# The prologue of a convolution, attention and expert kernel: group norm, first block and setup products in another order

## The chip, the cores and the metric

The kernel runs on one core of one Trainium2 chip. The metric is device microseconds of one execution; lower is better. Of the kernel before there are three timed runs and one profiled execution.

## The reference

The input x is (4, 128, 64, 64), four images of 128 channels and 4096 places. Two layers follow each other.

- Layer 0: x is normalised in 32 groups of 4 channels (group norm). Three 1x1 convolutions with bias and PReLU give e1 and e2 (64 channels each) and asm (128 channels). Scores are e1 transposed times e2, 4096 x 4096 per image; softmax over the second axis; the weighted sum of asm is added to x.
- Layer 1: with the places as tokens, layer norm, then attention with queries, keys and values of 128 features, added; then layer norm and a routed expert layer (64 experts, each takes its 8 top tokens by a softmax over the tokens; pooled, two dense layers with an exact GELU, scattered back), added.

The core of what concerns the change:

```python
xn = (g - m) / jnp.sqrt(s + eps)                  # mean, variance over 4 channels and all places
e1, e2, asm = prelu(w @ xn + b)                   # w1 64x128, w2 64x128, wa 128x128
out = softmax(e1.T @ e2, axis=2) @ asm.T          # per image
```

## The kernel before, in words

An image is held as 128 partitions (channels) x 4096 columns and is worked in 8 blocks of 512 columns (NB = 8, BLK = 512). Attention takes one block of 512 queries as a row (8 rows), and in each row 8 groups (NG = 8) of four key chunks of 128, that is one block of keys per group.

**PSUM** has 8 banks, in three pools: `sc` (scores, two tiles of two banks), `av` (products, two tiles of one bank, av0 and av1), `ms` (everything else, two tiles of one bank, taken in turn).

**Order of the work.** Instructions are traced by Python and then ordered on each engine by a scheduler, which takes the earlier traced first among those that it holds to be ready. `tc.keep_in_program_order` pins an instruction behind the one traced before it on its engine; `tc.no_sync_barrier` keeps the order between what is traced ahead of it and after it. Work that goes beside attention is written as generators, and a step of a generator (`next`) is traced after each group. `keep_busy(k)` traces k pinned matmuls of the identity into a spare PSUM tile (filler, so that TensorE does not stand idle); `FIRST_FILL` has the counts of the prologue.

**The prologue, in traced order** (function `tile_unshifted`):

1. Lines 118 to 152: the first image's 8 blocks are loaded, four by the SP queue and four by the ACT queue, then the small parameters on the same two queues (a12, wa, ba, aa on ACT; the others on SP). Lines 154 to 181: GpSimd builds the identity and averaging matrices; `avg_g` takes the mean of a group, `off_g` subtracts it.
2. Line 1221: `first_a`, 25 fillers. Lines 1222 and 1223: the first product of `weights_qk` (L503) and its copy on ACT (L505), the first ACT instruction that needs a table.
3. `group_norm(0, first_x)`: eight bn_stats (L220), bn_aggr (L223); then a channel's deviation from its group's mean and the mean itself by two matmuls into one bank (L230, L231); DVE copies both and forms the squared deviation plus the channel's variance (L233 to L237); a third matmul averages that (L240). `inv_sqrt` (L185) adds eps on DVE, takes the power -1/2 on GpSimd (L191) and does one Newton step with three DVE instructions (L192 to L196). Fillers `first_b` stand before the third matmul. Then come the other products of `weights_qk` with `first_e` and `first_c`.
4. `conv(0, first_x)`, a generator. First `normed` (L291) gives xk of block 0. Then, for block n: `both` (L378, pe: e1 and e2 together; L380, pa: asm by four 128-column pieces), ACT adds the bias (ye, L330), PReLU on DVE (te, L283, and L285), the next block's `normed`, and a yield; DVE adds ba (L363), PReLU into the values (L283, L285), and two yields. For block 0 the query and the keys are written in place by three L285 instructions, and ACT copies the query to the other 64 partitions (L344). For the other blocks the keys are placed by two DMAs of the SP queue (L348), and e1 goes to memory (L349).
5. Two `next` of that generator are traced before two setup products: `pgate` (L1239, copied to gate by L1240) and the transposes of a bias, `pw` (L1244, copied to w1bT by L1248). Both take a tile of the `ms` pool, as pe and pa do. `first_d` fillers stand between.
6. `stage(0, 0, ..., ahead=first_conv, pace=(4, 3))`: four more `next` of the convolution, then the attention of image 0. In the first row, after each group, three `next` are traced (so one block).

**A step of attention** (`attention`, L587 to 655): for group g the score matmuls (L625; 64 rows of the array each, the two halves of a key pair on different rows), exp on ACT (L634), the products of the group before (`rows_products`, L559) and the sum of exps on DVE (L646, L649).

Of the kernel before, what the change touches and what calls it, by code (L numbers as in the profile page):

```python
# [9 lines left out]
F32 = mybir.dt.float32  # L10
AF = mybir.ActivationFunctionType
# [15 lines left out]
def tile_unshifted(  # L27
# [91 lines left out]
    for n in range(NB):  # L119
        part = bass.ts(n, BLK)  # L120
        (nc.sync, nc.scalar)[n % 2].dma_start(out=first_x[:, part], in_=x[0][:, part])

    def const_load(name, shape, src, queue=None, pool=None):
        t = (pool or const).tile(shape, F32, tag=name, name=name, bufs=1)
        (queue or nc.scalar).dma_start(out=t, in_=src)
        return t
# [58 lines left out]
    def inv_sqrt(dst, var, eps, k, name):  # L185

        v = small.tile([P, SUB], F32, tag="iv", name=f"{name}_v")
        y = small.tile([P, SUB], F32, tag="iy", name=f"{name}_y")
        z = small.tile([P, SUB], F32, tag="iz", name=f"{name}_z")
        nc.vector.tensor_scalar(v[:, :k], var, eps, None, op0=ALU.add)  # L190
        nc.gpsimd.tensor_tensor(y[:, :k], v[:, :k], mhalf[:, :k], op=ALU.pow)  # L191
        nc.vector.tensor_mul(z[:, :k], y[:, :k], y[:, :k])  # L192
        nc.vector.scalar_tensor_tensor(
            z[:, :k], in0=z[:, :k], scalar=-0.5, in1=v[:, :k], op0=ALU.mult, op1=ALU.mult
        )
        nc.vector.scalar_tensor_tensor(  # L196
            dst, in0=z[:, :k], scalar=1.5, in1=y[:, :k], op0=ALU.add, op1=ALU.mult
        )
# [4 lines left out]
    def group_norm(b, first=None):  # L203
        st = prep.tile([P, NB, 6], F32, tag="gn_st", name=f"gn_st{b}")

        def pair(i):
            if i == NB // 2:
                return []
            if first is not None:
                return [first[:, bass.ts(2 * i + h, BLK)] for h in range(2)]  # L210
            return [
                load_block("xs", x_of(b, 2 * i + h), f"g{b}_{2 * i + h}", 4) for h in range(2)
            ]

        coming = pair(0)
        yield
        for i in range(NB // 2):
            blocks, coming = coming, pair(i + 1)
            for h in range(2):
                nc.vector.bn_stats(out=st[:, 2 * i + h, :], in_=blocks[h])  # L220
            yield
        mv = prep.tile([P, 2], F32, tag="gn_mv", name=f"gn_mv{b}")
        nc.vector.bn_aggr(out=mv, in_=st.rearrange("p n s -> p (n s)"))  # L223
        yield
        ab = const.tile([P, 2], F32, tag=f"gn{b}", name=f"gn{b}")
        if first is None:
            yield from group_norm_turned(b, mv, ab)
            return
        pm = ms_tile(f"gn_pm{b}")
        nc.tensor.matmul(pm[:, 0:1], lhsT=off_g, rhs=mv[:, 0:1], start=True, stop=True)  # L230
        nc.tensor.matmul(pm[:, 1:2], lhsT=avg_g, rhs=mv[:, 0:1], start=True, stop=True)  # L231
        d = prep.tile([P, 2], F32, tag="gn_d", name=f"gn_d{b}")
        nc.vector.tensor_copy(d[:, 0:1], pm[:, 0:1])  # L233
        nc.vector.scalar_tensor_tensor(
            d[:, 1:2], in0=d[:, 0:1], scalar=d[:, 0:1], in1=mv[:, 1:2], op0=ALU.mult, op1=ALU.add
        )
        nc.vector.tensor_copy(ab[:, 0:1], pm[:, 1:2])  # L237
        yield
        pv = ms_tile(f"gn_pv{b}")
        nc.tensor.matmul(pv[:, 0:1], lhsT=avg_g, rhs=d[:, 1:2], start=True, stop=True)  # L240
        inv_sqrt(ab[:, 1:2], pv[:, 0:1], GN_EPS, 1, f"gn{b}")
        gn[b] = ab
        yield
# [42 lines left out]
                o, in0=part(y), scalar=0.0, in1=part(t), op0=ALU.max, op1=ALU.add  # L286
            )

    def normed(b, xb, name):
        xn = block_tile("xn", name)  # L290
        nc.vector.tensor_scalar(  # L291
            xn, xb, gn[b][:, 0:1], gn[b][:, 1:2], op0=ALU.subtract, op1=ALU.mult
        )
        return xn

    keys, values, queries, resid = {}, {}, {}, {}
# [7 lines left out]
    def conv(b, whole=None, cols=None):  # L304
# [9 lines left out]
            return whole[:, bass.ts(n, BLK)]  # L314

        xb = block(0)
        coming = normed(b, xb, f"xk{b}_0")
        xb = block(1)
        yield
        for n in range(NB):  # L320
            xn = coming
            pe = ms_tile(f"pe{b}_{n}")
            if cols:
                for part in cols:
                    nc.tensor.matmul(pe[part, :], lhsT=w12[:, part], rhs=xn, start=True, stop=True)  # L325
            else:
                pa = ms_tile(f"pa{b}_{n}")
                both(xn, pe, pa)
            y, t = block_tile("ye", f"ye{b}_{n}"), block_tile("te", f"te{b}_{n}")
            nc.scalar.activation(y, pe, AF.Identity, bias=b12)  # L330
            places = [kA[h * CR : (h + 1) * CR, bass.ts(n, SUB // 2), :] for h in range(2)]

            def chunks(h):
                return lambda z: z[CR:, :].rearrange("c (p h t) -> c p h t", h=2, t=P)[:, :, h, :]

            if whole is not None and n == 0:

                queries[b, 0, n] = q = block_tile("q", f"e1_{b}_{n}")
                prelu(
                    [(q[:CR, :], lambda z: z[:CR, :])]  # L340
                    + [(places[h], chunks(h)) for h in range(2)],
                    y, t, a12,
                )
                nc.scalar.copy(q[CR:, :], q[:CR, :])  # L344
            else:
                prelu([(y, lambda z: z)], y, t, a12)
                for h in range(2):
                    nc.sync.dma_start(out=places[h], in_=chunks(h)(y))  # L348
                nc.sync.dma_start(out=e1[b][n], in_=y[:CR, :])  # L349
            if n + 1 < NB:  # L350
                coming = normed(b, xb, f"xk{b}_{n + 1}")
            yield
            if cols:
                pa = ms_tile(f"pa{b}_{n}")
            for s in range(SUB if cols else 0):
                for part in cols:
                    nc.tensor.matmul(  # L357
                        pa[part, bass.ts(s, P)], lhsT=xn[:, bass.ts(s, P)][:, part], rhs=wa,
                        start=True, stop=True,
                    )  # L360
            y2, t2 = block_tile("ye", f"ya{b}_{n}"), block_tile("te", f"ta{b}_{n}")
            y3 = y2.rearrange("p (s c) -> p s c", c=C)
            nc.vector.tensor_tensor(  # L363
                y3, pa.rearrange("p (s c) -> p s c", c=C),
                ba.unsqueeze(1).to_broadcast([P, SUB, C]), op=ALU.add,
            )
            prelu(
                [(vT[:, bass.ts(n, SUB), :], lambda z: z.rearrange("p (s c) -> p s c", c=C))],
                y2, t2, aa,
            )  # L370
            if n + 2 < NB:
                xb = block(n + 2)
            yield
            yield

    def both(xn, pe, pa):

        nc.tensor.matmul(pe, lhsT=w12, rhs=xn, start=True, stop=True)  # L378
        for s in range(SUB):
            nc.tensor.matmul(  # L380
                pa[:, bass.ts(s, P)], lhsT=xn[:, bass.ts(s, P)], rhs=wa, start=True, stop=True
            )
# [116 lines left out]
    def weights_qk():  # L499
        wT = []  # L500
        pqk = sc_tile("pwq_pwk")
        for i, w in enumerate((wqT, wkT)):
            nc.tensor.matmul(pqk[:, i, :P], lhsT=w, rhs=unfold, start=True, stop=True)  # L503
            t = block_tile("te", f"wT{i}")[:, :P]
            nc.scalar.copy(t, pqk[:, i, :P])  # L505
            wT.append(t)
# [638 lines left out]


    FILL = (3, 0, 3, 3, 15, 4, 2, 3)
    FIRST_FILL = (25, 3, 2, 2, 2)

    def keep_busy(k, name, t=None):  # L1150

# [66 lines left out]
    nc.sync.dma_start(out=w1b, in_=a["weight1"][:, D1 - 1, :])  # L1218
    cent = block_tile("ye", "cent")[:, :P]
    nc.gpsimd.tensor_scalar(cent, ident, -1.0 / C, None, op0=ALU.add)  # L1220
    keep_busy(FIRST_FILL[0], "first_a")
    projections = weights_qk()
    next(projections)
    first_norm = group_norm(0, first_x)
    for step in range(NB // 2 + 4):
        next(first_norm, None)
        if step == NB // 2 + 2:
            keep_busy(FIRST_FILL[1], "first_b")
    next(projections)
    keep_busy(FIRST_FILL[4], "first_e")  # L1230
    next(projections)
    keep_busy(FIRST_FILL[2], "first_c")
    tc.no_sync_barrier()
    run(projections)
    first_conv = conv(0, first_x)
    next(first_conv)
    next(first_conv)
    pw = ms_tile("pgate")
    nc.tensor.matmul(pw[:, :E], lhsT=cent, rhs=gate, start=True, stop=True)  # L1239
    nc.scalar.copy(gate, pw[:, :E])  # L1240
    keep_busy(FIRST_FILL[3], "first_d")
    pw = ms_tile("pw")
    for c in range(NHC):
        nc.tensor.transpose(  # L1244
            pw[:, bass.ts(c, E)], w1b.rearrange("e (p c) -> e c p", c=NHC)[:, c, :],
            ident[:E, :E],
        )
    nc.scalar.copy(w1bT.rearrange("p c e -> p (c e)"), pw[:, : NHC * E])  # L1248
    run(query(0, 0, 0))
    tc.no_sync_barrier()  # L1250

# [90 lines left out]
                load_part(0, 0, 1, 3, 1)  # L1342
                load_part(1, 1, 1, 2, 1)

    stage(0, 0, chain(group_norm(1), conv(1)), (1, 0), ahead=first_conv, pace=(4, 3))
    packing = pack_weights()
    stage(1, 0, chain(group_norm(2), attn_keys(0), mix_values(0)), (0, 1))
    stage(0, 1, chain(group_norm(3), conv(2, cols=SCORE_COLS[1])), (2, 0), skip=1)
# [743 lines left out]
```

## Time and profile before

| | us |
|---|---|
| median of 3 runs (lowest to highest) | 3227.67 (3226.14 to 3229.38) |
| the profiled execution | 3227.37 |
| its span | 3225.6 |
| TensorE busy in the span | 3200.6 |
| first image's transfers landed | 9.01 |
| first pe matmul starts | 14.41 |
| first score matmul starts | 19.39 |
| first product (av) starts | 27.21 |
| last group of the first row with a projection: its pe starts | 60.00 |

Times within the span count from its start. A profile's chain lists, in order of time, the work that ended last and what released each piece: start, duration, engine, tile and line. A timeline lists instructions by start, with the engine's idle time before them and what ended it. TensorE's records are pipelined: the durations of two that follow each other overlap.

A steady group without a projection beside it takes 1.72 us for eight score matmuls and 3.43 us for sixteen products. A group with one takes 1.06 (pe), 0.89 (pa), 1.92 and 3.43.

### The profile page before, as it was taken

What the parts mean: (1) busy time and instruction counts of PE and PEld (TensorE: products, weight loads), DVE (VectorE), ACT (ScalarE), POOL (GpSimd) and SP (SyncE); (2) the same over time, 40 slices, a digit from 0 to 9 for tenths busy, and PEclk for the clock granted to TensorE, in tenths of its full rate; (3) what the DMA queues carried; (4) which work ended last, traced back from release to release, by engine and by line L of the source; (5) the groups of instructions that cost most, each with busy time, mean ns of one, the idle gap of its engine ahead of it and who ended that gap; (6) DMA issues with size and microseconds to landing.
All of it is one profiled execution on the core that took longest, in us unless ns stands there. A gap on an engine that the chain in (4) does not pass through costs nothing.

```text
span 3225.6 us, 49325 instructions
## 1 busy us (share of the span) xinstructions
PE 3200.6 (99%) x19620; PEld 1574.1 (49%) x19620; DVE 2127.5 (66%) x4237; ACT 1275.0 (40%) x1571; POOL 386.8 (12%) x422
## 2 busy tenths in 40 slices
PE   9999999999999999999999999999999999999997
PEld 5444444444555544444554444444445454546663
DVE  7665577556675668755775657775776566676564
ACT  3344444443433345443333334444333333343341
POOL 0111113210000003240000001332100002010001
PEclk9999999999999999999999999999999999999999
DMA  3121244223232212311221111231131111122159
GB/s 91 49 53 30 76 104 121 77 87 86 73 86 82 63 49 47 79 33 27 53 47 27 37 30 40 78 79 25 44 70 37 37 24 37 24 69 93 34 182 387
DMA packets 370128, 222.90 MB, mean 69 GB/s; under 512 B 275424, under 2 KB 300128, under 8 KB 366560
## 3 DMA queue, kind: packets, MB, share of 16 engines
q1 hardware_dynamic: 365616, 208.51, 24.1%
q10 hardware_dynamic: 3760, 10.10, 0.8%
q8 instruction: 156, 2.56, 0.3%
q0 software_dynamic: 512, 1.05, 0.1%
q14 instruction: 84, 0.69, 0.1%
HBM read 159.75 MB, written 97.19 MB: 80 GB/s over the span
## 4 chain that ended last, share of the span: by engine, by line
PE 98%; DVE 1%; DMA 0%; issue 0%; ACT 0%; SPq 0%; DVEq 0%; POOL 0%; ACTq 0%
PE ps L625 41%; PE av L559 27%; PE av L587 24%; PE pq L528 1%; PE pv L772 1%; PE pe L378 1%; PE po L1457 0%; PE pa L380 0%; PE pa L357 0%; PE pe L325 0%; PE ph L1423 0%; PE pg L828 0%; PE px L1537 0%; DMA first_x<-in_x_dram 0%; PE av_pht L1434 0%; DVE w L1544 0%
## 5 line engine op out<-in xcount | busy, mean ns | idle before, releaser
L634 ACT ACTIVATE pt<-ps 128x1024 f32<-128x1024 f32 x1024 | 1020.9, 1023 | 1466.3 <-PE ps L625 1390.3
L625 PE MATMUL ps<-q,t 128*64 128x512 f32 x4096 | 934.3, 592 | 0.0
L559 PE MATMUL av<-pt,asm 64*128 64x512 f32 x4096 | 922.3, 589 | 0.0
L649 DVE TENSOR_TENSOR sacc<-sacc,pt 128x1024 f32<-128x1024 f32 x448 | 587.3, 1311 | 294.2 <-ACT pt L634 269.7
L587 PE MATMUL av<-pt,tt 128*64 128x256 f32 x3072 | 636.2, 379 | 0.0
L559 PEld LDWEIGHTS av<-pt,asm 64*128 64x128 f32 x4096 | 401.0, 187 | 479.1 <-issue 477.8
L573 DVE TENSOR_TENSOR tt<-pt 128x512 f32<-128x512 f32 x512 | 354.7, 693 | 354.0 <-ACT pt L634 336.5
L625 PEld LDWEIGHTS ps<-q,t 128*64 128x64 f32 x4096 | 305.1, 137 | 482.4 <-issue 451.7
L587 PE MATMUL av<-tt,mixed 128*64 128x256 f32 x2048 | 525.6, 379 | 0.0
L587 PEld LDWEIGHTS av<-pt,tt 128*64 128x64 f32 x3072 | 356.0, 137 | 270.3 <-issue 135.0
L625 PE MATMUL ps<-e,e 64*128 64x512 f32 x2048 | 486.1, 592 | 0.0
L625 PEld LDWEIGHTS ps<-e,e 64*128 64x128 f32 x2048 | 196.2, 187 | 235.8 <-issue 232.6
L587 PE MATMUL av<-tt,tt 128*64 128x256 f32 x1024 | 304.7, 379 | 0.0
L587 PE MATMUL av<-pt,mixed 128*64 128x256 f32 x1024 | 304.6, 379 | 0.0
L587 PEld LDWEIGHTS av<-tt,mixed 128*64 128x64 f32 x2048 | 280.5, 137 | 8.8
L191 POOL TENSOR_TENSOR l_y<-l_v,mhalf 128x4 f32<-128x4 f32 x64 | 64.9, 1013 | 1631.6 <-DVE l_v L190 1631.2
L574 DVE TENSOR_TENSOR pt<-tt,pt 128x256 f32<-128x256 f32 x512 | 219.9, 430 | 17.0
L575 DVE TENSOR_TENSOR tt<-pt 128x256 f32<-128x256 f32 x512 | 219.5, 429 | 17.0
L587 PEld LDWEIGHTS av<-pt,mixed 128*64 128x64 f32 x1024 | 140.2, 137 | 65.4 <-DVE pt L574 0.3
L587 PEld LDWEIGHTS av<-tt,tt 128*64 128x64 f32 x1024 | 140.1, 137 | 4.7 <-DVE tt L575 0.3
L666 POOL TENSOR_TENSOR u<-u,c 128x512 f32<-128x512 f32 x32 | 40.7, 1271 | 555.6 <-ACT c L665 555.6
L646 DVE TENSOR_TENSOR sacc<-pt,pt 128x1024 f32<-128x1024 f32 x32 | 39.1, 1221 | 53.1 <-ACT pt L634 53.1
(323 smaller groups left out, 1755.4 us busy)
## 6 DMA issues: line engine op xcount, KB each, us to landing
wp<-in_weight_dram SPq DMA_DIRECT2D x128, 256.0 KB, 4.2
w<-wp SPq DMA_DIRECT2D x10, 1024.0 KB, 13.5
w<-wp SPq DMA_DIRECT2D x17, 512.0 KB, 9.1
xq<-in_x_dram SPq DMA_DIRECT2D x32, 256.0 KB, 3.9
rb<-inv SPq DMA_DIRECT2D x32, 256.0 KB, 3.3
xT<-xt SPq DMA_DIRECT2D x128, 64.0 KB, 2.2
ak<-xT SPq DMA_DIRECT2D x32, 256.0 KB, 3.6
t<-kt SPq DMA_DIRECT2D x128, 64.0 KB, 2.2
```

Source lines behind the costliest of these rows:

```text
L191: nc.gpsimd.tensor_tensor(y[:, :k], v[:, :k], mhalf[:, :k], op=ALU.pow)
L378: nc.tensor.matmul(pe, lhsT=w12, rhs=xn, start=True, stop=True)
L559: nc.tensor.matmul(avs[b, 0, n][r], lhsT=values[b, 0][rows, j, :], rhs=pt[rows, h, :], start=(j == 0), stop=(j == NJ - 1),)
L573: nc.vector.tensor_sub(tt[:, 0:2, :], p4[:, :, 1, :], p4[:, 0, :, :])
L574: nc.vector.tensor_add(p4[:, 0, 1, :], tt[:, 1, :], p4[:, 0, 0, :])
L575: nc.vector.tensor_sub(tt[:, 2, :], p4[:, 1, 0, :], p4[:, 0, 1, :])
L587: nc.tensor.matmul(av[bank][bass.ts(half, HC), slot, :], lhsT=lhsT, rhs=rhs, start=first, stop=final, skip_group_check=True,)
L625: nc.tensor.matmul(ps[part, h, :], lhsT=key[:, part], rhs=q[rows, :], start=True, stop=True,)
L634: nc.scalar.activation(pt, ps, AF.Exp, scale=scale)
L646: nc.vector.tensor_add(sums[b, n], pts[0], pts[1])
L649: nc.vector.tensor_add(sums[b, n], sums[b, n], pt)
L666: nc.gpsimd.tensor_add(u, u, c0)
```

## The change

1. A copy of one element per partition on ACT, pinned behind the four image loads of the ACT queue, so that the activation table is loaded there; a DVE memset writes its source.
2. Group norm of image 0: the mean goes to a tile of the `sc` pool. The channel's variance goes into PSUM by a matmul of its own with `start=True, stop=False`; ACT squares the deviation out of PSUM (Square), and a second matmul of the same group adds its average.
3. `inv_sqrt` with k = 1: -0.5 (var + eps) is formed by a separate DVE instruction that does not need the power, and two DVE instructions follow the power instead of three. The three later group norms of the kernel use it too.
4. Block 0: `normed` in two halves of 256 columns, and its pe matmul in two halves. `both` is split into `both_e` and `both_a`, and for block 1 a yield is put between them. The ba addition of block 0 is pinned.
5. The two products of `weights_qk` with wq and wk are pinned. All fillers go to av0 instead of an `sc` tile; `first_b` falls from 3 to 1, and the fillers between the setup products go. (The list has four entries now, and `first_d` is the former `first_e`.)
6. Five `next` of the convolution, not two, are traced before the setup products, the fifth ending with pe of block 1. The setup products go to av1, pinned, their two copies behind them. pace (4, 3) becomes (0, 3). The three steps traced after group g of the first row are then those of block g + 1 (for group 0, without its pe, which stands ahead of the setup products), where they were those of block g + 2.

```diff
+    early = pools["prep"].tile([P, 2], F32, tag="early", name="early", bufs=1)
+    nc.vector.memset(early[:, 0:1], 0.0)
+    tc.keep_in_program_order(nc.scalar.copy(early[:, 1:2], early[:, 0:1]))
...
         nc.gpsimd.tensor_tensor(y[:, :k], v[:, :k], mhalf[:, :k], op=ALU.pow)
+        if k == 1:
+            nc.vector.tensor_scalar(v[:, 1:2], var, eps, -0.5, op0=ALU.add, op1=ALU.mult)
+            nc.vector.scalar_tensor_tensor(
+                z[:, :1], in0=y[:, :1], scalar=v[:, 1:2], in1=y[:, :1], op0=ALU.mult,
+                op1=ALU.mult,
+            )
+            nc.vector.scalar_tensor_tensor(
+                dst, in0=z[:, :1], scalar=1.5, in1=y[:, :1], op0=ALU.add, op1=ALU.mult
+            )
+            return
...
         nc.tensor.matmul(pm[:, 0:1], lhsT=off_g, rhs=mv[:, 0:1], start=True, stop=True)
-        nc.tensor.matmul(pm[:, 1:2], lhsT=avg_g, rhs=mv[:, 0:1], start=True, stop=True)
+        pa = sc_tile(f"gn_pa{b}")[:, 0, :]
+        nc.tensor.matmul(pa[:, 0:1], lhsT=avg_g, rhs=mv[:, 0:1], start=True, stop=True)
+        pv = ms_tile(f"gn_pv{b}")
+        nc.tensor.matmul(pv[:, 0:1], lhsT=avg_g, rhs=mv[:, 1:2], start=True, stop=False)
         d = prep.tile([P, 2], F32, tag="gn_d", name=f"gn_d{b}")
-        nc.vector.tensor_copy(d[:, 0:1], pm[:, 0:1])
-        nc.vector.scalar_tensor_tensor(
-            d[:, 1:2], in0=d[:, 0:1], scalar=d[:, 0:1], in1=mv[:, 1:2], op0=ALU.mult, op1=ALU.add
-        )
-        nc.vector.tensor_copy(ab[:, 0:1], pm[:, 1:2])
-        yield
-        pv = ms_tile(f"gn_pv{b}")
-        nc.tensor.matmul(pv[:, 0:1], lhsT=avg_g, rhs=d[:, 1:2], start=True, stop=True)
+        nc.scalar.activation(d[:, 0:1], pm[:, 0:1], AF.Square)
+        nc.vector.tensor_copy(ab[:, 0:1], pa[:, 0:1])
+        yield
+        nc.tensor.matmul(pv[:, 0:1], lhsT=avg_g, rhs=d[:, 0:1], start=False, stop=True)
...
-                both(xn, pe, pa)
+                both_e(xn, pe, 2 if whole is not None and n == 0 else 1)
+                if whole is not None and n == 1:
+                    yield
+                both_a(xn, pa)
...
-    FIRST_FILL = (25, 3, 2, 2, 2)
+    FIRST_FILL = (25, 1, 2, 2)
...
-    next(first_conv)
-    next(first_conv)
-    pw = ms_tile("pgate")
-    nc.tensor.matmul(pw[:, :E], lhsT=cent, rhs=gate, start=True, stop=True)
-    nc.scalar.copy(gate, pw[:, :E])
-    keep_busy(FIRST_FILL[3], "first_d")
-    pw = ms_tile("pw")
+    for _ in range(5):
+        next(first_conv)
+    pgate, pw = setup[:, 0, :E], setup[:, 0, P : P + NHC * E]
+    tc.keep_in_program_order(
+        nc.tensor.matmul(pgate, lhsT=cent, rhs=gate, start=True, stop=True)
+    )
     for c in range(NHC):
...
-    nc.scalar.copy(w1bT.rearrange("p c e -> p (c e)"), pw[:, : NHC * E])
+    tc.keep_in_program_order(nc.scalar.copy(gate, pgate))
+    tc.keep_in_program_order(nc.scalar.copy(w1bT.rearrange("p c e -> p (c e)"), pw))
...
-    stage(0, 0, chain(group_norm(1), conv(1)), (1, 0), ahead=first_conv, pace=(4, 3))
+    stage(0, 0, chain(group_norm(1), conv(1)), (1, 0), ahead=first_conv, pace=(0, 3))
```

## The prediction

> **What bounds the kernel now.** I read the page first: part 1 and the chain (part 4). TensorE carries nearly the whole span, and the chain of work that ended last is matmuls.
>
> ```profile
> PE 3200.6 (99%) x19620; PEld 1574.1 (49%) x19620; DVE 2127.5 (66%) x4237; ACT 1275.0 (40%) x1571; POOL 386.8 (12%) x422
> ...
> PE 98%; DVE 1%; DMA 0%; issue 0%; ACT 0%; SPq 0%; DVEq 0%; POOL 0%; ACTq 0%
> ```
>
> So an edit of the prologue can win only the time by which the unbroken row of matmuls starts earlier, and it keeps that if nothing later in the row gives it back. The busy times by stretch say how short the place is.
>
> ```profile
> 0.00:10.40 10.40, 8.42 (x51) 8.37 (x52) 5.14 (x9) 0.34 (x1) 4.30 (x20) 1.00 0.69 227
> 10.40:27.20 16.80, 15.96 (x84) 10.30 (x86) 12.40 (x28) 7.72 (x14) 2.44 (x7) 1.00 0.22 53
> ...
> 400.00:3100.00 2700.00, 2700.00 (x16668) 1326.44 (x16666) 1804.76 (x3774) 1077.32 (x1295) 328.72 (x343) 1.00 0.23 58
> ```
>
> Columns: stretch, length, then busy time of PE, weight load, DVE, ACT, POOL. From 400 to 3100 us PE is never idle. Up to 10.4 us the first image's transfer decides, and its PE work is filler on `ident`. The change can act on 10.4 to 27.2 us and on the rest of the first row, to 67. "Busy" hides much there: it contains filler and slow matmuls. The chain of that window, in order of time (start, us, what), shows it.
>
> ```profile
> 2.20 6.81 DMA first_x<-in_x_dram
> ...
> 10.87 0.35 PE gn_pm L230 x2
> 11.22 0.22 PE gn_pm L231 x2
> 11.45 0.78 PE first_b L1155 x6
> 12.22 0.13 PE gn_pv L240 x2
> ...
> 14.41 1.12 PE pe L378 x2
> ...
> 17.91 0.38 ACT w1bT L1248
> 18.29 0.04 issue
> 18.34 1.12 PE pe L378 x2
> 19.46 1.05 PE ps L625 x2
> 20.51 1.09 PE pa L380 x8
> 21.60 1.91 PE ps L625 x6
> ```
>
> Two things to see. Block 1's projection (pe, 18.34) waits for a copy of the setup product w1bT, whose buffer it takes. And the first scores run in pieces: 2 instructions in 1.05 us, then block 1's pa, then 6 in 1.91, where 8 together take 1.72 in the steady row. The timeline tells why the second half of the scores is late: the copy of the query (L344) stands behind w1bT on ACT.
>
> ```profile
> 17.91 0.37 ACT L1248 COPY w1bT<-pw 128x256 f32<-128x256 f32 x1 [0.91 <-PE pw L1244]
> 18.30 0.62 ACT L344 COPY e<-e 64x512 f32<-64x512 f32 x1
> ```
>
> **What the Trainium skill says.** "ScalarE: Activation LUTs", What ACT_TABLE_LOAD costs: a load takes about 1283 ns; an ACTIVATE has a fixed part of 186 ns, and some 93 more for each pointer operand. The trace agrees on the load (1283 ns, 10.06 to 11.34); a 128x512 Identity with a bias takes 687 ns and a 128x64 copy 212. "TensorE: Matmul & The Clock Gate", Part 3: matmuls in different row groups run at once; the trace shows it, 0.43 us for a pair of 64-row passes against 0.525 for one alone. "PSUM — Partial Sum Buffer", PSUM bank collisions: two engines must be kept off one bank, whatever the columns. The trace agrees: the copy of column 0 of gn_pm starts at 11.49, though its matmul ended at 11.22, because L231 wrote column 1 until 11.45.
>
> **The change, part by part**, on the profiled execution (3227.37 us, span 3225.6, so 1.77 around it; the median is 3227.67).
>
> *Table load early.* The load and a tiny copy go on ACT behind its four image DMA issues, which end at 2.67, and before the next issue at 5.10. 1.28 + 0.2 ends at 4.15: nothing is delayed, 0.95 us of slack (the copy's wait is for a DVE memset, and DVE is idle to 4.92); were it gone, six small parameter loads would be late, the first needed (wa) at 15 us. The first copy moves from 11.36 to about 10.8, so ACT is free for the new Square.
>
> *Variance in PSUM.* Off the path go the wait for L231 (11.22 to 11.49), a DVE copy and a scalar_tensor_tensor (to 11.90). In their place is a Square: 0.16 (copy's fixed part) to 0.28 (the skill's pointer form); I take 0.26, 11.26 to 11.52. PE now does three means, 0.22 each, from 10.87, to 11.53, then one filler (2 passes of 0.13, instead of 6), and the last matmul starts at 11.79, not 12.06: **gain 0.27**. PE's own queue ends last, not the Square. Behind the Square on ACT stands the copy of the wk product, which waits for a later matmul anyway; behind the last matmul on PE stand that product and fillers. If Square is not in the set that Copy and Exp share, two further loads of 1.28 stand here.
>
> *Two steps after the power.* One of three dependent DVE steps (13.23, 13.42, 13.62) goes: **gain 0.19**. The added step (0.16) runs beside the power on GpSimd (0.58). The later images' group norms take this branch too, with the same number of DVE steps, under full PE cover.
>
> *First block in halves.* The 0.54 us pass becomes two of about 0.3, so pe starts 0.25 earlier; but its second half queues behind the first, and the filler first_c ends at 13.78: it starts at 13.80. The end of pe moves from 15.54 to about 14.95: **0.6 in all so far**, of the 0.71 on paper.
>
> *Block 1 ahead of the setup products.* Moved: three steps of the first convolution's generator, with the ba addition, the value prelu and pe of block 1. pe1 needs block 0's buffer, which ACT's ye frees at 14.98 + 0.69 = 15.67; PE is at pa until 15.75. So pe1 15.75 to 16.80, gate and four transposes 0.27 + 0.55 (their rows, fillers off) to 17.62. Their copies are in the av bank, pinned behind the query copy, and delay nobody on PE (av is first needed after 20). The query copy follows the first of three L285 passes, which start 0.6 earlier (16.22, not 16.82): 16.8 to 17.42; the third ends at 17.81. Scores then run whole: 17.84 to 19.6 with a switch of row mode (1.92 against 1.72 in the first row, so 0.2). Then pa1 1.09 to 20.7.
> Then av of group 0 may go at once (exp of its first pair by about 20.3): 0.2 + 3.43 to 24.3. The keys of block 1 pass ACT ye at about 18.4 (behind w1bT's copy), DVE te and ye', and two DMAs: landed by about 23.4. Scores 1, 1.72 to 26.0; pe2 and pa2, 0.2 + 1.94, to 28.1. Before, the same list of work (to the end of av 0) ended at 30.74: **gain 2.6**, of which 1.24 is the pairing of scores (1.05 + 1.91 less 1.72), 0.6 the norm, the rest the wait for w1bT and its fillers.
>
> *What the row gives back.* pace (4,3) becomes (0,3), so block g+1, not g+2, is projected in the step of group g. Before, from the end of a pe (31.86) to landed keys it took 5.2 us: ye to 32.59, te, ye' to 34.31, the second key DMA issued at 34.99, 2.0 to landing, 37.0; scores 3 used them at 39.98, 3.0 us later. That cover is gone. In the new step, behind a pe stand pa (0.89), a switch (0.2) and the previous group's av (3.43): 4.5 us, 0.7 short. But the program's order on each engine is not the text's order: the trace has pa1 between two halves of scores, and the second xk ahead of the first te. Where scores lack keys, the next block's pe and pa (1.94) can be put before them. So each of six groups costs 0 to 0.7; I take 0.13: **loss 0.8**. SP's queue gets the key stores as before, behind the row's xq load, and the query spread (two issues, 1.1 us) stands before block 2's in time to be clear.
>
> Sum: 2.6 - 0.8 = 1.8; 3227.37 - 1.8 = 3225.6; on the median's level (0.3 higher) **3225.8**.
>
> **The rivals.** What this kernel's measurement can tell from no change is about 0.2%, 6.5 us; all but one case lie inside it.
> (A) The forecast, 3225.8; half the chance, 0.52.
> (B) Given back: scores still split by pa1 (1.24 lost again), and 0.3 in each of six groups: 2.6 - 1.24 - 1.8 = -0.4, so 3228.1. For it: the 5.2 us chain against 4.5, and DVE's 2.54 us sums that can stand before a te. Against: the query copy is no longer the late one. 0.28.
> (C) The slower end, one mechanism: the keys' lead. If the order stays scores, av, pe, pa in every step, as the trace of before has it from 25.4 on, the lead falls by one group, 7.29, from +3.0 to -4.3, and PE waits 4.3 us before scores in six groups: 26 - 2.6 = +23, 3251. It decides from 1.5 us of waiting a group ((6.5 + 2.6)/6). Against: the reordering just named. 0.07.
> (D) Square sits in another table set: two loads of 1.28 on the path take 2.6 from the forecast: 3228.4. The trace has no Square, and the skill's list of functions common to all sets leaves it out. 0.05.
> (E) Nothing is given back and steps of the row need fewer switches: 2.6 + 6 x 0.2: 3223.9. 0.08, of it 0.02 for a rearranged later stage that gains over 0.2%.
>
> **How the numbers follow.** A, B, D and E are within 0.2%: 0.91; faster 0.02; slower 0.07 from C. The range holds A, B, D and E with their bounds: below, a gain of 3.8 and a run's spread (3226.1 to 3229.4, so 0.6 of a median): 3223.3; above, B with 0.7 in a few groups: 3229.3. C is left out.
>
> **What would show it.** Right: the table load near 2.7; gn_pv ended by 12.1, xk by 13.4, pe of block 1 near 15.8 before the gate, scores of group 0 as 8 together from 17.8, av of group 0 ended near 24.3. Wrong: a second table load; PE waits before scores between 23 and 67 in the waits; groups of the first row longer than 7.5 us; the end of the first row's last pe not 1 to 2.6 us earlier than 61.05. I would be wrong most in the row: the head's gain rests on rows of the trace, the row's loss on an order I have not seen.

## The result, and the profile after

The changed kernel is slower: 3265.66 us median (3265.29 to 3266.63, four runs) against 3227.52 (3226.14 to 3229.38, four runs), a ratio of 1.0118 (95% interval 1.0106 to 1.0131), 38.1 us. The forecast was 3225.8, its range ended at 3229.3. The profiled execution took 3266.63 us, its span is 3264.9.

First part 1, the chain's shares and the scores' group of the page of after.

```profile
PE 3220.7 (99%) x19616; PEld 1597.0 (49%) x19616; DVE 2125.7 (65%) x4237; ACT 1276.1 (39%) x1573; POOL 388.3 (12%) x422
...
PE 97%; DMA 1%; DVE 1%; ACT 0%; issue 0%; DVEq 0%; SPq 0%; ACTq 0%
...
L653 PE MATMUL ps<-e,e 64*128 64x512 f32 x2048 | 511.3, 598 | 18.9 <-DMA e<-ye 18.9
```

The shares look as before; only the last line tells something new. The score matmuls of layer 0's first convolution now stand idle 18.9 us for a DMA that writes keys (e<-ye). The waits of TensorE count them.

```profile
PE ps L653 <- DMA e<-ye: 18.9, 7, 2.7
```

Seven waits, the longest 2.7 us; the kernel before has no such line. But 18.9 is half of 38.1. The busy times by stretch of after (columns as before: PE, weight load, DVE, ACT, POOL; then the granted clock) show where the whole of it lies. The last line is of the kernel before.

```profile
10.40:27.20 16.80, 13.89 (x69) 10.60 (x70) 11.03 (x24) 5.46 (x12) 2.34 (x7) 0.87 0.25 66
27.20:67.30 40.10, 31.95 (x107) 17.93 (x106) 17.05 (x24) 8.31 (x10) 0.00 (x0) 0.88 0.11 28
...
400.00:3100.00 2700.00, 2700.00 (x16574) 1319.36 (x16572) 1802.93 (x3737) 1077.75 (x1297) 331.05 (x345) 1.00 0.23 59
```

```profile
27.20:67.30 40.10, 40.10 (x190) 19.64 (x188) 31.31 (x44) 14.46 (x17) 0.00 (x0) 1.00 0.23 55
```

From 400 to 3100 us PE is never idle, as before. Between 27.2 and 67.3 it is busy 31.95 of 40.10 us, where it was busy all of it with 190 matmuls; now there are 107, and the granted clock is 0.88. The filler `busy_a` that ends the attention stage starts at 3166.8, not at 3127.8. So 39 us are lost before it, 38 of them by the end of the first row, and nothing comes back later.

The timeline of PE in after shows one group of that row.

```profile
32.77 1.12 PE L401 MATMUL pe<-xk,w 128*128 128x512 f32 x2
33.73 1.05 PE L406 MATMUL pa<-wa_sb,xk 128*128 128x128 f32 x8
34.72 1.12 PE L587 MATMUL av<-pt,asm 64*128 64x512 f32 x2
38.57 2.68 PE L653 MATMUL ps<-e,e 64*128 64x512 f32 x7 [2.73 <-DMA e<-ye]
...
41.52 4.75 PE L587 MATMUL av<-pt,asm 64*128 64x512 f32 x13
46.20 1.12 PE L401 MATMUL pe<-xk,w 128*128 128x512 f32 x2
```

From pe to pe it is 13.43 us (32.77 to 46.20), 7.29 before. Behind pe and pa only two of the sixteen matmuls of the products stand ahead of the waiting scores (34.72); the others come among and behind them, though their inputs have long been there. The chain of after tells what the scores wait for (start, us, what).

```profile
32.84 1.07 PE pe L401 x2
...
33.93 0.70 ACT ye L349
...
35.74 0.60 DVE ye L298
...
36.37 2.06 DMA e<-ye
...
38.57 2.68 PE ps L653 x7
```

The block projected at 32.8 is the one whose scores are due next: projection, bias, PReLU and DMA now lie on the path of each group, 5.8 us from pe to the scores.

And the granted clock (the third number from the end) behind three of the seven waits, in stretches of after that begin near the wait's end:

```profile
38.50:43.50 5.00, 4.93 (x14) 2.95 (x15) 1.53 (x2) 2.05 (x2) 0.00 (x0) 0.66 0.15 34
...
65.00:70.00 5.00, 4.57 (x20) 2.70 (x21) 1.66 (x2) 1.94 (x2) 0.00 (x0) 1.00 0.19 43
...
90.50:95.50 5.00, 5.00 (x15) 2.84 (x17) 1.23 (x1) 1.89 (x2) 0.00 (x0) 0.66 0.12 27
```

Six of seven waits are followed by a mean clock of 0.65 to 0.67 over 4.5 or 5 us: a third of 5 us lost, 1.7 us a wait (3.4 us at half). After the fourth wait (65 us) the clock stayed at 1.00, and that group (59.73 to 71.38) took 11.65 us, not 13.4.

Last, the prologue, in the timeline of ACT in after.

```profile
2.71 1.28 ACT L125 ACT_TABLE_LOAD   x1 [2.71 <-issue]
...
11.31 0.17 ACT L250 ACTIVATE gn_d<-gn_pm 128x1 f32<-128x1 f32 x1 [0.28 <-PE gn_pm L244]
```

The table load is early, the Square took 0.17 us, and no second load stands in the prologue. From the end of bn_aggr to the first xk it is 2.74 us (10.77 to 13.51), 3.09 before: the norm gives 0.35. The scores of group 0 run as eight together, from 18.99.

My theory after this: the loss is the keys' lead. In pace (0, 3) a block is projected in the group before its scores, and PE waits; the half clock behind the waits is the rest. Rivals: another part of the change (setup products, fillers, block 0) costs it; or the order of the matmuls costs it and the lead would have been enough; or the time is DVE's and the DMAs only come last. "Group" below is the time from pe to pe in the first row.

### The profile page after: what moved, and what is told of

The parts are those of the page before. It is cut to its first block, busy times and chain, and to the rows that moved or that the text cites. A ratio compares the mean times of both kernels' runs of the same rounds, so it can differ in the third digit from the quotient of the medians.

```text
span 3264.9 us, 49325 instructions
## 1 busy us (share of the span) xinstructions
PE 3220.7 (99%) x19616; PEld 1597.0 (49%) x19616; DVE 2125.7 (65%) x4237; ACT 1276.1 (39%) x1573; POOL 388.3 (12%) x422
## 4 chain that ended last, share of the span: by engine, by line
PE 97%; DMA 1%; DVE 1%; ACT 0%; issue 0%; DVEq 0%; SPq 0%; ACTq 0%
PE ps L653 41%; PE av L587 27%; PE av L615 24%; PE pq L556 1%; PE pv L800 1%; PE pe L401 1%; DMA e<-ye 0%; PE pa L376 0%; PE pe L341 0%; PE pg L856 0%; PE ph L1454 0%; PE po L1488 0%; DMA t<-x 0%; DMA out_dram<-t 0%; PE pa L406 0%
## 5 line engine op out<-in xcount | busy, mean ns | idle before, releaser
L587 PE MATMUL av<-pt,asm 64*128 64x512 f32 x4096 | 953.9, 592 | 0.0
L587 PEld LDWEIGHTS av<-pt,asm 64*128 64x128 f32 x4096 | 421.7, 188 | 473.8 <-issue 467.0
L653 PE MATMUL ps<-e,e 64*128 64x512 f32 x2048 | 511.3, 598 | 18.9 <-DMA e<-ye 18.9
L653 PEld LDWEIGHTS ps<-e,e 64*128 64x128 f32 x2048 | 207.7, 188 | 256.8 <-issue 251.2
```

The lines of the kernel that those rows point to most:

```text
L587: nc.tensor.matmul(avs[b, 0, n][r], lhsT=values[b, 0][rows, j, :], rhs=pt[rows, h, :], start=(j == 0), stop=(j == NJ - 1),)
L653: nc.tensor.matmul(ps[part, h, :], lhsT=key[:, part], rhs=q[rows, :], start=True, stop=True,)
```

## Experiment 1: the lead alone given back

```diff
-    stage(0, 0, chain(group_norm(1), conv(1)), (1, 0), ahead=first_conv, pace=(0, 3))
+    stage(0, 0, chain(group_norm(1), conv(1)), (1, 0), ahead=first_conv, pace=(2, 3))
```

> The changed kernel with pace (2,3) in place of (0,3): two more steps of the first convolution stand ahead of the first scores, so block g + 2 is again projected in the step of group g; all else of the change stays. Theory (the keys' lead is the whole loss): no wait of scores for the key DMAs, groups of the first row back at 7.3 us, and 3224 to 3227 us. Rival (the new norm, table load, pinned products or buffers lose the time): the loss stays, over 3250.

Measured: 3227.1 us (3226.21 to 3229.67, 13 runs), before on the same chip 3227.44; ratio 1.0 (0.9991 to 1.0008). No score of the first row waits for a key DMA, and PE is busy 40.10 of 40.10 us from 27.2 to 67.3. So the lead is the whole loss, and no other part of the change costs anything that can be measured (the interval is some 2.6 us to either side). But no gain remains: 3227.1 is at the upper end of the theory's range. The timeline of PE in this kernel tells a part of why.

```profile
19.96 1.16 PE L406 MATMUL pa<-wa_sb,xk 128*128 128x128 f32 x8 [0.94 <-DVE ya L382]
21.05 1.99 PE L653 MATMUL ps<-e,e 64*128 64x512 f32 x8
```

The two extra steps put pa of block 1 ahead of the scores of group 0, where it waits 0.94 us for DVE; those scores start at 21.05. Scores 1 start at 25.50, against 25.39 before: the prologue's gain is spent by then. In this profile the clock was also at half from 12.6 to 16.0 us; the setup products start 1.5 us later than in a profile where it was not (18.08 against 16.61 in experiment 9), so the order of pa is not the only reason.

## Experiment 2: the lead alone taken from the kernel before

```diff
-    stage(0, 0, chain(group_norm(1), conv(1)), (1, 0), ahead=first_conv, pace=(4, 3))
+    stage(0, 0, chain(group_norm(1), conv(1)), (1, 0), ahead=first_conv, pace=(1, 3))
```

> The kernel before with only pace (4,3) made (1,3), so that block g + 1 is projected in the step of group g; nothing else of the change. Theory: the loss appears by itself: scores wait some 2.7 us for key DMAs in each of six or seven groups, 13.4 us a group, and 3260 to 3267 us. Rival: the kernel before keeps 3227 to 3235, because it is the other parts that break it.

Measured: 3264.57 us (3263.72 to 3265.57, 4 runs), ratio 1.0117 (1.0102 to 1.0133). One number in the kernel before brings 37.1 us, nearly all of the change's 38.1, with the same groups of 13.4 us (pe at 30.10, 43.53, 56.92) and the same line in its waits.

```profile
PE ps L625 <- DMA e<-ye: 18.0, 7, 2.7
```

With experiment 1 this settles the part: it is the lead, whatever the prologue.

## Experiment 3: the waits filled

Twelve pinned fillers stand before the scores of groups 1 to 7 of the first row. They write into the scores' own PSUM tile, which the scores then overwrite.

```diff
                     ps = sc_tile(f"ps{nm}_{n}_{p}")
+                    if (b, layer, n) == (0, 0, 0) and g > 0 and p == 2 * g:
+                        keep_busy(12, f"wait{g}", ps)
```

> The changed kernel with 12 fillers (identity by identity, 0.26 us each) in the scores' own PSUM tile ahead of the scores of groups 1 to 7 of the first row, where TensorE waits for keys. The fillers also take away the single av matmul that the changed order puts there. Theory (each wait also halves the granted clock for one window after it, 1.7 us a group, and the lone av costs about 1.2): clock 1.0 through the row, about 11 us a group, 3247 to 3253 us. Rival (the wait is all, the clock costs nothing): only the lone av's cost goes, 3257 or more.

Measured: 3254.89 us (3253.46 to 3255.36, 4 runs), ratio 1.0085 (1.0069 to 1.01), a little above my range. The timeline of PE:

```profile
29.57 1.12 PE L401 MATMUL pe<-xk,w 128*128 128x512 f32 x2
...
31.42 2.84 PE L1185 MATMUL ps<-ident 128*128 128x128 f32 x24
35.26 2.25 PE L655 MATMUL ps<-e,e 64*128 64x512 f32 x7 [1.00 <-DMA e<-ye]
...
41.31 1.12 PE L401 MATMUL pe<-xk,w 128*128 128x512 f32 x2
```

The keys come no earlier: from the end of pa (31.42, where the fillers begin) to the scores it is 3.84 us; in after it is 3.85 (34.72 to 38.57). But the clock is 1.00 in the whole first row, and the group takes 11.74 us, as the one group of after that kept its clock (11.65). So of 38.1 us, some 10.8 (3265.66 less 3254.89) are the half clock behind the waits, which agrees with six waits of 1.7, 10.2. (The profile of after also has half clock in the prologue, 1.6 us, and that of this experiment has not; the 10.8 may hold some of that.) The rest is 27.4 over before, and six groups of 4.45 more (11.74 - 7.29) are 26.7 of it.

The Trainium skill's "TensorE: Matmul & The Clock Gate", Part 1 (The HAM clock gate, and HAM oscillation) describes this: a free-running window of about 3.4 us, half the clock after an idle one, full clock again after a busy one, and as the rule no idle gaps above 3.4 us. The 3.4 us at half clock agree. But the gaps here were only 2.65 to 2.75 us, and six of seven were enough, so the rule's margin is too wide for this row.

The trace of after shows what told the seventh from the others. The half-clock stretches of the first row begin at 26.39, 40.04, 53.70, 77.59, 91.24 and 104.90 us. The steps between them are 4, 4, 7, 4 and 4 times 3.413 us, so all lie on one grid of 3.413 us. Here are four stretches of that grid: the one ahead of the second half clock, the one ahead of the third, and the two that the fourth wait touches.

```profile
36.63:40.04 3.41, 1.47 (x6) 0.96 (x7) 1.25 (x3) 0.00 (x0) 0.00 (x0) 1.00 0.34 77
50.28:53.70 3.42, 1.71 (x7) 1.08 (x9) 1.12 (x2) 0.00 (x0) 0.00 (x0) 1.00 0.34 77
60.52:63.94 3.42, 2.21 (x11) 1.15 (x9) 2.36 (x5) 0.69 (x1) 0.00 (x0) 1.00 0.00 0
63.94:67.35 3.41, 1.92 (x8) 1.23 (x10) 0.87 (x2) 0.17 (x1) 0.00 (x0) 1.00 0.36 82
```

PE was idle for 1.94 and 1.71 us of the first two, 57 and 50%. The grid cuts the fourth wait (2.70 us) into 1.21 and 1.49 us, 35 and 44%, and the clock stayed full. The other four stretches ahead of a half clock were idle for 64 to 79%. Experiment 2 agrees: five stretches with 57 to 80% idle were followed by half clock, and a wait of 2.68 us that its grid cut into 1.07 and 1.60 us was not. So what counted in these rows was the idle share of a stretch, with the limit between 47% (1.60 us, experiments 2 and 4) and 50%, and not the length of the gap alone. The grid lies differently in each profiled execution.

## Experiment 4: the keys without a DMA

The keys of blocks 1 to 7 of the first convolution are written in place by two DVE instructions on 64 partitions, as block 0's are. It takes about 2 us of transfer out of the chain and gives DVE more to do.

```diff
-                prelu([(y, lambda z: z)], y, t, a12)
-                for h in range(2):
-                    nc.sync.dma_start(out=places[h], in_=chunks(h)(y))
+                if whole is not None:
+                    prelu(
+                        [(places[h], chunks(h)) for h in range(2)]
+                        + [(y[:CR, :], lambda z: z[:CR, :])], y, t, a12,
+                    )
+                else:
...
```

> The changed kernel, short lead kept, but in the first convolution blocks 1 to 7 write their keys in place with two 64-partition DVE instructions, as block 0 does, instead of two DMAs out of ye. Theory (the DMAs, 2.65 us from the first issue, are what the lead no longer covers): the wait falls from 2.7 to about 1 us a group (ye 0.69, te 0.49, two times 0.53 less pa 0.89), the clock stays up, and 3229 to 3236 us. Rival (the order of the matmuls alone costs the time): 3250 or more.

Measured: 3237.55 us (3237.14 to 3238.99, 5 runs), ratio 1.0034 (1.002 to 1.0047), above my range again. The timeline over all engines:

```profile
29.22 0.68 DVE L388 TENSOR_TENSOR ya<-pa,ba_sb 128x512 f32<-128x512 f32 x1
29.94 0.87 DVE L298 SCALAR_TENSOR_TENSOR e<-ye,te 64x256 f32<-64x256 f32 x2
...
30.50 2.34 PE L659 MATMUL ps<-e,e 64*128 64x512 f32 x8 [1.60 <-DVE e L298]
```

The wait is now for DVE, 1.60 us, because the ba addition (0.68) runs between te (28.82, 0.49) and the key writes; I had expected about 1 (the terms that I listed add to 1.35, and the ba addition was not among them). It is short enough that the clock stays 1.00. The group is 9.32 us (pe 26.89 to 36.21). So the transfer, with the clock it costs, is 28.1 of 38.1 us, and the short lead costs 10 even without a transfer: ACT and DVE alone are too long for it.

## Experiments 5, 6 and 9: is there a gain in the prologue?

The lead is restored behind group 0 instead of ahead of it: six steps of the convolution follow group 0, three each later group (pace (0, 3, 3)). Experiment 6 adds two fillers to the first 25, experiment 9 takes six away.

```diff
-                for _ in range(pace[1]):
+                for _ in range(pace[1] + (sum(pace[2:]) if g == 0 else 0)):
...
-    stage(0, 0, chain(group_norm(1), conv(1)), (1, 0), ahead=first_conv, pace=(0, 3))
+    stage(0, 0, chain(group_norm(1), conv(1)), (1, 0), ahead=first_conv, pace=(0, 3, 3))
```

```diff
-    FIRST_FILL = (25, 1, 2, 2)
+    FIRST_FILL = (27, 1, 2, 2)
```

```diff
-    FIRST_FILL = (25, 1, 2, 2)
+    FIRST_FILL = (19, 1, 2, 2)
```

> The changed kernel, in which group 0 of the first row alone is followed by six steps of the first convolution, not three (pace (0,3) with three more for group 0): the scores of group 0 still come straight after the setup products, and from group 1 on block g + 2 is projected in the step of group g. Theory (the prologue's gain is there, and the lead alone hid it): no wait for key DMAs beyond 0.5 us, av of group 0 started by about 25.2 instead of 27.2, and 3224.5 to 3226.5 us. Rival (pace (2,3) gave nothing back because the prologue itself gains nothing): the same time as before within 0.5 us.

> The same with 27 first fillers instead of 25. Theory (with 25, TensorE stood idle from 9.7 to 10.2 and around 10.7, and the granted clock was 0.5 from 12.9 to 16.1 in two of four profiles): no half clock in the prologue, scores of group 0 start at 17.5 to 18, and 0 to 1.5 us less than with 25. Rival (the half clock comes by the chance of the execution, whatever the fillers): no difference in the median.

> The kernel of e5 with 19 first fillers instead of 25, so that TensorE stands idle about 1.5 us longer before the group norm's first matmul. Theory (that idle time is what halves the clock from 13 to 16 us): the half clock is there, scores of group 0 start at about 19 us, and the time is that of e5 plus 0 to 1 us, as e5's profile had the half clock too. Rival (the half clock is a matter of the execution's chance): the clock may be 1.0 there, and the time does not depend on the count.

| | us (range, 13 runs each) | before, same chip | ratio, 95% |
|---|---|---|---|
| 5, six steps | 3227.38 (3226.01 to 3228.82) | 3227.28 | 0.9999 (0.999 to 1.0007) |
| 6, and 27 fillers | 3226.87 (3225.64 to 3228.3) | 3227.28 | 0.9997 (0.9989 to 1.0006) |
| 9, and 19 fillers | 3227.26 (3226.17 to 3230.57) | 3227.86 | 0.9999 (0.9991 to 1.0007) |

None can be told from the kernel before. Experiment 5 came out on its rival's side: 3227.38 us, not 3224.5 to 3226.5, and av of group 0 starts at 27.25 in its profile, not at 25.2. In the profiles of after, of experiment 1 and of experiment 5 the clock was at half from about 13 to 16 us (in after a mean of 0.54 over 13.0 to 16.4, so 1.6 us lost); it was full in those of 6 and 9. I had thought that short idle time of PE before 11 us decides it. Experiment 9 has more of it (0.9 us before the first product of `weights_qk`, against 0.5 in 5) and kept its clock, so that idle time alone does not decide it; more on this at the end of "Why the prediction was wrong".

In 9, scores 0 start at 17.40 (the forecast said 17.84), and av of group 0, with the work that the forecast listed, ends at 29.5 against 30.74; `busy_a` starts at 3126.6, 1.2 us earlier than before. In 6 av of group 0 ends at 29.55, but `busy_a` starts at 3127.3, only 0.5 earlier. So in these two profiles the head gains 1.2 us, 0.04%, and 0.5 to 1.2 of it is left at the end of attention; that is under what the times can show. Of the 1.4 us missing to the forecast's 2.6 the trace of 9 shows these pieces: the eight scores of group 0 take 2.38 us (17.40 to 19.78), 0.46 over the 1.92 that the forecast allowed; pa of block 2 waits 0.16 us for DVE; scores 1 wait 0.48 us for keys, and one of their weight loads 0.29 us more.

## Experiment 7: the order that the forecast assumed

In the first row the products of the group before are traced ahead of the scores; the rest is after as it is.

```diff
+                early = (b, layer, n) == (0, 0, 0)
+                if early:
+                    products()
                 for p in (2 * g, 2 * g + 1):
...
-                products()
+                if not early:
+                    products()
```

> The changed kernel, short lead kept, but in the first row the products of the group before are traced ahead of a group's scores, which is the order that the forecast took for granted. Theory (the failed step is the order of the matmuls, not the budget of keys against av): the wait falls from 2.7 to 0.3 to 1.0 us a group, the clock stays up, and 3226 to 3232 us. Rival (the short lead can't be covered by av at all): 3240 or more.

Measured: 3237.86 us (3237.18 to 3240.54, 6 runs), ratio 1.0032 (1.002 to 1.0044): between what the theory and the rival expected. The order is as assumed now (pe, pa, 16 av together, 8 scores together), and the head is as forecast: pa of block 2 ends at 28.26, forecast 28.1. So the order was worth 27.8 us. (This and the 28.1 of experiment 4 are not two parts of the loss: each takes most of the same waits away, in its own way.) But a group still takes 9.2 us (pe 26.31, 35.54, 44.72). The timeline:

```profile
26.65 2.56 DVE L681 TENSOR_TENSOR sacc<-sacc,pt 128x1024 f32<-128x1024 f32 x2 [1.94 <-ACT pt L665]
...
29.12 0.48 DVE L296 TENSOR_SCALAR te<-ye,a 128x512 f32<-128x512 f32 x1
...
33.02 2.59 PE L656 MATMUL ps<-e,e 64*128 64x512 f32 x8 [1.06 <-DMA e<-ye]
```

ACT's ye runs from 27.47 to 28.16; te starts at 29.12, because DVE is at the two exp sums (26.65 to 29.21), and scores wait 1.06. That DVE takes its queue strictly in order is what the Trainium skill's "TensorE: Matmul & The Clock Gate" says (Part 1, engine queue depths); the trace agrees, te follows the sums.

## Experiment 8: and the sums out of the way

Experiment 7, with the first row's exp sums traced one group later, behind the products.

```diff
+                if early:
+                    products()
+                    while late:
+                        nn, pp = late.pop()
+                        add_sums(nn, pp)
...
+                elif early and g < NG - 1:
+                    late.append((n, pts))
```

> The kernel of e7 (short lead, products of the group before ahead of a group's scores), in which the first row's sums of exps are traced one group later, so that te of the next keys does not stand behind them on DVE (in e7 ye ended at 28.16 and te began at 29.12). Theory (in the assumed order the keys are late by DVE's queue and by the budget): the wait falls from 1.0 to 0 to 0.3 us a group, a group takes 8.0 to 8.4 us instead of 9.2, and 3230 to 3234 us. Rival (the sums don't matter, the two DMAs set the time): 3237 to 3238 us as e7.

Measured: 3232.42 us (3230.89 to 3235.06, 21 runs), before 3227.86, ratio 1.0014 (1.0008 to 1.0021): the theory's range. The timeline:

```profile
28.23 0.49 DVE L296 TENSOR_SCALAR te<-ye,a 128x512 f32<-128x512 f32 x1 [3.35 <-ACT ye L349]
...
32.13 2.59 PE L670 MATMUL ps<-e,e 64*128 64x512 f32 x8
...
32.74 0.72 PEld L670 LDWEIGHTS ps<-e,e 64*128 64x128 f32 x5 [0.34 <-DMA e<-ye]
...
34.65 1.12 PE L401 MATMUL pe<-xk,w 128*128 128x512 f32 x2
```

te starts 0.03 us after ye (ended 28.20), the products (28.29, sixteen together) cover nearly all of the transfer of the first keys, and PE stands idle only 0.14 us before the scores. The group is still 8.31 us (26.34 to 34.65), 1.02 over 7.29. Some 0.7 of that lies in the scores themselves: from their start to the next pe it is 2.52 us (32.13 to 34.65), where the group before, whose keys were all there, took 1.81 (24.53 to 26.34). Their third weight load waits 0.34 us for the second key transfer, and behind it the matmuls of a key pair no longer start together: the first four start at 32.13, 32.64, 32.74 and 33.07, in the group before at 24.53 and 24.54, 24.96 and 24.97. The other 0.3 lies between the start of the products and the scores (3.84 us against 3.54). Both come from the transfers: 3.54 us behind the start of the products would be 31.83, and the second keys are there only by 32.74, 0.9 later.

## Why the prediction was wrong

The step that failed is "What the row gives back", with its "loss 0.8". It put 0.13 us on each of six groups; a group of after took 6.1 us more (13.4 less 7.29).

| kernel | order in the row | group, us | over before, us |
|---|---|---|---|
| forecast | products ahead of scores | 7.42 | -1.8 |
| experiment 8 | so, sums later | 8.31 | +4.6 |
| experiment 7 | so | 9.2 | +10.6 |
| experiment 4 | scores ahead, no transfer | 9.3 | +10.1 |
| experiment 3 | scores ahead, waits filled | 11.74 | +27.5 |
| after | scores ahead | 13.4 | +38.1 |

- **Order, the larger error.** I put the products of the group before between pa and the scores, and reasoned that the program's order on an engine is not the text's, so that even the next block's pe and pa could go ahead of scores without keys. The trace of before had scores ahead of products in every group; rival C named that and got 0.07. In after only two product matmuls pass the scores. Experiment 7 measures this error: 27.8 us (3265.66 less 3237.86), the half clock included.
- **Budget, the smaller one.** Even in the assumed order a group lost 1.9 us, not 0 to 0.7. The 5.2 us chain was read from a group of before in which DVE was idle when ye ended; DVE's sums (named under rival B, and left out of the sum) put te 0.96 us later. Without them the chain is again 5.3 us (experiment 8: pe ended at 27.47, the second keys were there by 32.74), against a cover of 4.4 (to 31.83): 0.9 short, close to the 0.7 that I had worked out and then cut to 0.13 because pe and pa might go first. They did not.
- **Rival C's price was right, its sum was not.** It gave 4.3 us a group in six groups; 4.45 was measured with the clock held (experiment 3). Not all of that is waiting: from the end of pa to the scores it is 3.84 us, and the scores and products behind take 0.7 more than before (35.26 to 41.31, 6.05, against 5.35). It had +26 - 2.6 = +23; missing were the half clock, 10.8, and the head, which loses instead of gaining in this order (below).
- **The head, forecast 2.6.** Right for its own order: in experiment 7 the list of work ends at 28.26, 2.5 us earlier than before. In after it ends with pa of block 2 at 34.72, 4.0 later than before, 6.6 later than forecast: scores 1 wait 2.65 us for keys (landed 25.03, forecast 23.4) with no product ahead of them, the clock behind that wait costs 1.7, and the half clock from 13 to 16 us 1.6. Of the 0.7 that is left, 0.45 is in the eight scores of group 0 (18.99 to 21.36, 2.37, where the forecast had 1.92).
- **After's 38.1 in one sum:** head 4.0, five groups of 13.05 on average (32.77 to 98.02 over 5) less 7.29, 28.8, and the group behind the last projection, 10.35 less 5.15 (1.72 + 3.43), 5.2. Together 38.0, of the 39.0 by which `busy_a` starts later in this profile. The last 1.0 comes in the second row, ahead of the next projection (162.87, 123.88 before), and was not followed.
- **Right:** table load early at no cost; Square in the shared set, at 0.17 us near the lower of my bounds (the page "ScalarE: Activation LUTs" has a fixed part of 0.186, What ACT_TABLE_LOAD costs); norm 0.35 of the 0.46; scores of group 0 together from 17.4 to 17.5 where the clock held; the setup products delay nobody.
- **The signs of being wrong** were the ones that came: waits before scores, groups over 7.5 us. What failed was the weight: I assumed an order that no trace had shown, against the one that the trace of before did show, and that one got 7 in 100.

What stays open is the half clock of the prologue. It is in the profiled executions of after and of experiments 1 and 5, and not in those of before and of the other seven. After and experiments 1, 3, 4, 5, 7 and 8 have the same prologue to that point, so the program alone does not decide it. The grid of experiment 3 fits: in the three with the half clock a stretch of it begins at 9.16 to 9.73 us, in experiments 3, 4, 7 and 8 at 7.47 to 8.18 (there counted back from the half clock at the kernel's end). Experiment 6, with two more fillers, has it at 9.54 and kept its clock, as its theory expected; experiment 9 has it at 7.62, so it was no test of that theory. But these are single profiles, and the stretch ahead of the half clock was idle for only 22 to 23%, so the share of the first row is not the whole rule. That stretch holds the group norm's matmuls of one column; whether such matmuls count for less was not tried. How often it comes in executions that were not profiled is not known; the three profiled ones took 0.9 to 1.0 us more than the medians of their kernels.

## What to carry to other kernels

When an edit shortens the lead of a producer, take the order of before as the order of after and price the wait so; a scheduler that reorders is a hope until a trace shows it. Add to each wait on a tuned matmul row what its clock does afterwards: here it was 40% more. A gain at the head of an unbroken row is worth its microseconds once, a lead that is short by one group is paid in every group.

## What the runs showed of the hardware

- Idle gaps of TensorE of 2.65 to 2.75 us between dense matmuls were followed by 3.4 us at half clock in six of seven cases in after; gaps of 1.0 to 1.7 us (experiments 2, 3, 4 and 7) were not. The half clock came on a grid of 3.413 us, behind every stretch of the first row that was idle for at least half (1.71 to 2.74 us; six in after, five in experiment 2), and behind none that was idle for less (up to 1.60 us).
- A Square of one element per partition out of PSUM took 0.17 us on ACT in after, and no table load stands between it and the one that the first copy brings.
- Where the keys of one group come by two transfers, the wait for the second is in the row of the weight load (0.34 us, experiment 8), not in that of the matmul, and the eight scores took 2.52 us instead of 1.81.
